# The last FFN's first batch: rows turned by VectorE's blocks instead of TensorE, projections and queries of the last attention batch spread anew

## The chip, the cores and the metric

One Trainium2 chip, one core of it. The kernel is one launch. The metric is device time in microseconds (us). The kernel before took 2222.87 us, the median of 4 runs that lay between 2220.93 and 2227.34 us. Besides these there is one profiled execution, whose trace all durations below are taken from.

The engines are called as the profile calls them: PE is TensorE (matrix products, transposes by a product with the identity), PEld its weight loads, DVE is VectorE, ACT is ScalarE, POOL is GpSimd, and SP issues most of the DMAs.

## The reference

Four layers with a layer norm behind each, on 8 batches of 512 rows of 512 numbers, all in float32:

```python
x = _layernorm(x + _L0_attn_ref(x, ...))   # 16 heads of 32, causal
x = _layernorm(x + _L0_ffn_ref(x, ...))    # 8 experts, the best 2 for each row
x = _layernorm(x + _L1_attn_ref(x, ...))   # 8 heads of 64, keys and values shared by 4 heads
x = _layernorm(x + _L1_ffn_ref(x, ...))    # gate, up and down by integer weights, hidden width 1408
```

The change lies at the seam of the last two. The attention of layer 1 ends with `x + out @ Wo.T`, a residual and a layer norm. The last FFN is

```python
W = (wq.astype(jnp.float32) - 128) * scale[:, None]
gate = silu(x @ Wg.T); up = x @ Wu.T
y = (gate * up) @ Wd.T
```

## The kernel before

**Layer 1's attention.** `Attention1.batches` runs batches 0 to 7 one after the other. A batch has 4 groups of two heads, and for each group 4 tiles of 128 keys, so 16 units, taken two at a time: 8 rounds, numbered 0 to 7. `plan(b)` (L1745) fills a list `todo` with the extra work of each round. A round is written in this order: scores of its two units (L1702, PE into `sc`, then the exponential on ACT, L1705, into `p`); the sums over the units of the round before (`add`, L1713, DVE: none for a group's first unit, `total<-p,p` for its second, `total<-total,p` for its third and fourth); the round's list; the products of the round before (`product`, L1724, PE into `av`). Behind every group's last product, so in rounds 2, 4, 6 and in round 0 of the next batch, comes `normalise` (L1729): PE sums the rows of `total` into `rs` (L1732), ACT copies them to `r_inv` (L995), DVE takes the reciprocal (L1735) and multiplies `av` with it (L1742, into `aoT`), and POOL adds `r_inv` to a running sum that guards the result (L998).

**The lists.** They hold the queries of the next groups (L1607), the output projection of the batch before, 128 rows at a time (`project`: PE L1670, DVE's residual L1676 and statistics L1684 and L1685; after the fourth tile POOL's `rstd`, L1688 and L1689), and the preparation of the next batch. The last batch, 7, has no next one. There the lists hold `split(0, c)` in rounds 0, 2, 4 and 6: it prepares the rows of batch 0 for the FFN. Their layer norm was done long before. `split` has 4 PE transposes of 128 x 128 (L1108), ACT's copy from PSUM to `x_high` (L1109), rounded to the type in which PE multiplies, and DVE's difference from PSUM to `x_low` (L1110). Queries 1, 2, 3 are in rounds 0, 1, 5, projections 0 to 3 of batch 6 in rounds 2, 3, 4, 7.

**Order.** In this stage the programs of PE, DVE, ACT and POOL are kept in the order in which they are written. Each engine takes its own instructions strictly in turn, so one that waits holds up all behind it on that engine. SP's DMAs are put in order by the scheduler.

**The tail.** After round 7 come the two last sums, the two last products, three of the four groups of projection 0 of batch 7, `normalise` of the last group, the remaining groups and projections, the norm of batch 6 and the residuals of batch 7.

**Turning rows otherwise.** Batches 2 to 7 of this attention, and batches 1 to 7 of the FFN, get their turned rows another way, `Turn`. DVE transposes 32 x 32 blocks (`blocks`, L88, one instruction of 128 x 512 for each tile of rows), four DMAs carry the result to DRAM (`out`, L93), and one brings it back (`back`, L96), all on SP's queue. For the next batch of the attention DVE's four instructions stand in round 3 and the first reader, the key product L1588, in round 6. Rows turned so come in another order of the 512 tokens; `by_tile` is the view that undoes this, in FFN by ACT's L1153 and DVE's L1154, which read `hT` in that view. FFN batch 0 reads plainly there, since `split` keeps the order.

**The FFN.** `IntegerFfn.batch` runs 11 hidden tiles in a batch: 8 + 8 products with `x_high` and `x_low` (L1143), then the halves of the hidden tile, then the output products (L1159). `parts` (L1094) makes the halves of later batches from the turned rows: ACT's copy and DVE's difference.

**Weights.** `weights.load` brings 2 units of the integer weights, `weights.convert` converts the pair before; both do nothing once `FIRST` = 20 units are on the core.

Of the kernel before, what the change touches and what calls it, by code (L numbers as in the profile page):

```python
# [9 lines left out]
F32 = mybir.dt.float32  # L10
# [4 lines left out]
ALU = mybir.AluOpType  # L15
# [3 lines left out]
P = 128  # L19
NB = 8  # L20
S = 512
D = 512
NT = S // P
ND = D // P
# [33 lines left out]
def in_order(tc, *engines):  # L58


    return tc.manual_schedule(engines={mybir.EngineType.PE, *engines})
# [11 lines left out]
class Turn:  # L73
# [11 lines left out]
    def blocks(self, room, t, x):  # L85

        out = room.rearrange("p (j t c) -> p j t c", t=self.n, c=32)[:, :, t, :]
        self.nc.vector.transpose(out, x.rearrange("p (j c) -> p j c", c=32))  # L88
# [708 lines left out]
class Tiles:  # L797
# [83 lines left out]
    def weights(self, i, c):  # L881
        at = self.ats[i]
        if i < N_FIXED:
            return self.w[:, at + c * 512 : at + (c + 1) * 512]
        return self.w[:, bass.ds(at + c * 512, 512)]
# [180 lines left out]
class IntegerFfn:  # L1066
# [13 lines left out]
        self.halves[b] = [pool.tile([P, ND, S], F32R, tag=f"rows{i}", name=f"x3_{part}")  # L1080
                          for i, part in enumerate(("high", "low"))]

    def blocks(self, b, t):

        if t == 0:
            self.room(b)
            self.turned = self.raw.tile([P, ND * S], F32, tag="turned", name="turned")
        turn = self.turns[b % 2]
        turn.blocks(self.turned, t, self.env.xs[b][:, t, :])
        if t == NT - 1:  # L1090
            turn.out(self.turned)
            turn.back(self.turned)

    def parts(self, b, c):  # L1094

        high, low = (half[:, c, :] for half in self.halves[b])
        x = self.turned[:, ts(c, S)]
        self.nc.scalar.copy(high, x)
        self.nc.vector.tensor_tensor(low, x, high.bitcast(F32), ALU.subtract)

    def split(self, b, c, ps):

        nc = self.nc
        if c == 0:
            self.room(b)
        high, low = self.halves[b]
        for t in range(NT):
            nc.tensor.transpose(ps[:, ts(t, P)], self.env.xs[b][:, t, ts(c, P)], self.env.ident)  # L1108
        nc.scalar.copy(high[:, c, :], ps)  # L1109
        nc.vector.tensor_tensor(low[:, c, :], ps, high[:, c, :].bitcast(F32), ALU.subtract)  # L1110

    def run(self, held_out, last_norm):
        tc, nc, weights = self.env.tc, self.nc, self.weights
# [21 lines left out]
    def hidden(self, b, c, held):  # L1135

        nc, vec, work, weights = self.nc, self.env.vec, self.work, self.weights
        g = self.p_gu.tile([P, S], F32, tag="g", name="ps_g1")
        u = self.p_gu.tile([P, S], F32, tag="u", name="ps_u1")
        for ps, w in ((g, weights(2 * c)), (u, weights(2 * c + 1))):  # L1140
            for dc in range(ND):
                for i, x in enumerate(self.halves[b]):
                    nc.tensor.matmul(ps, lhsT=w[:, ts(dc, P)], rhs=x[:, dc, :],  # L1143
                                     start=(dc, i) == (0, 0), stop=(dc, i) == (ND - 1, 1))
        sg = work.tile([P, S], F32, tag="sg", name="sg1", bufs=2)
        nc.scalar.activation(sg, g, AF.Silu, scale=vec[:, V_SG + c : V_SG + c + 1])
        hT = work.tile([P, S], F32, tag="hT", name="hT2", bufs=2)
        nc.vector.scalar_tensor_tensor(hT, u, vec[:, V_SU + c : V_SU + c + 1], sg, ALU.mult, ALU.mult)  # L1148
        high, low = (self.late.tile([P, S], F32R, tag=f"h{i}", name="h_late") if held else
                     work.tile([P, S], F32R, tag=f"h{i}", name="h_half", bufs=2) for i in range(2))  # L1150

        hT, *halves = [self.turns[0].by_tile(a, back) if b else a for a, back in ((hT, True), (high, False), (low, False))]
        nc.scalar.copy(halves[0], hT)  # L1153
        nc.vector.tensor_tensor(halves[1], hT, halves[0].bitcast(F32), ALU.subtract)  # L1154
        return high, low
# [381 lines left out]
class Attention1:  # L1537
# [94 lines left out]
        for part in (self.w_qkv[:, c, :], self.w_qkv[:, ND : ND + 2, ts(c, P)]):  # L1632
            self.nc.scalar.mul(part, part, self.nss[:, c : c + 1])

    def run(self, weights, split):

        with ExitStack() as phase:
            self.work = work = phase.enter_context(self.env.tc.tile_pool(name="c_work", bufs=1, reuse_waits="tile"))
            p_sc = phase.enter_context(self.env.tc.tile_pool(name="c_sc", bufs=2, space=PSUM, reuse_waits="tile"))
            p_av = phase.enter_context(self.env.tc.tile_pool(name="c_av", bufs=2, space=PSUM, reuse_waits="tile"))  # L1640
            with in_order(self.env.tc, mybir.EngineType.DVE, mybir.EngineType.Activation, mybir.EngineType.Pool):
                return self.batches(work, p_sc, p_av, weights, split)

    def batches(self, work, p_sc, p_av, weights, split):
        env, nc, guard, state, HD = self.env, self.nc, self.guard, self.state, self.HD
        xs = env.xs
        scale = 1.0 / math.sqrt(HD)
# [14 lines left out]
        def project(b, t):  # L1662
            ps = self.mm([P, D], "ps_o1")
            project_groups(b, t, ps, range(ND))
            residual(b, t, ps)
            statistics(b, t)
# [24 lines left out]
        def norm(b):  # L1691
            st = state.pop(b)
            for t in range(NT):
                x = xs[b][:, t, :]
                nc.vector.tensor_scalar(x, x, st["mv"][:, t, 0:1], st["rstd"][:, t : t + 1], ALU.subtract, ALU.mult)
# [49 lines left out]
        def plan(b):  # L1745


            todo = [[] for _ in range(ND * NT // 2)]
            here = pieces.pop(b)
            first, final = b == 0, b == NB - 1  # L1750
            if first:
                pieces[1] = self.prepare(1)
                todo[0] += [lambda t=t: pieces[1]["fetch"](t) for t in range(NT)]
            then = pieces.get(b + 1)
            if b:
                for t, i in enumerate((2, 3, 4, 7) if final else (2, 3, 4, 5)):
                    todo[i].append(lambda t=t: project(b - 1, t))
                if not final:
                    todo[6].append(lambda: norm(b - 1))
            for g, i in zip((1, 2, 3), (1, 3, 5) if first else (0, 1, 5) if final else (0, 1, 3)):  # L1760
                todo[i].append(lambda g=g: here["query"](g))
            if final:
                for c, i in enumerate((0, 2, 4, 6)):
                    todo[i].append(lambda c=c: split(0, c, self.mm([P, S], "ps_xT")))
            else:
                if first:

                    for t, i in ((2, 1), (3, 2)):
                        todo[i].append(lambda t=t: then["sum"](t))
                        todo[i + 2].append(lambda t=t: then["stat"](t))  # L1770
                for t, i in ((0, 1), (1, 2)) if first else ((0, 0), (1, 1), (2, 1), (3, 2)):
                    todo[i].append(lambda t=t: then["add"](t))
                if first:
                    todo[4].append(then["deviations"])

                    todo[5].insert(0, then["norm"])
                    todo[6] += [lambda c=c: then["turn"](c) for c in range(ND)]
                else:
                    todo[2].append(then["deviations"])
                    todo[3].append(then["norm"])  # L1780
                    todo[3] += [lambda t=t: then["blocks"](t) for t in range(NT)]
                todo[6].append(then["key"])
                todo[7] += [then["value"], lambda: then["query"](0)]
                if b + 2 < NB:
                    after = pieces[b + 2] = self.prepare(b + 2)
                    todo[7] += [lambda t=t: after["fetch"](t) for t in range(NT)]
            for i in (7,) if first else (1, 7) if final else (5, 7):
                todo[i] += [weights.convert, lambda: weights.load(work, 2, weights.FIRST)]
            return todo

        last = []
        for b in range(NB):
            for i, thunks in enumerate(plan(b)):
                units = [(b, u // NT, u % NT) for u in (2 * i, 2 * i + 1)]
                ps = [score(*unit) for unit in units]
# [12 lines left out]
        b = NB - 1  # L1808
# [16 lines left out]
def usual_pass(tc, ins, held_out):  # L1825
    nc = tc.nc
    with ExitStack() as ctx:
# [4 lines left out]
        with tc.tile_pool(name="a_mm", bufs=2, space=PSUM) as p_mm, ExitStack() as attn1_ctx:  # L1832
            with tc.tile_pool(name="routes", bufs=1, side="right") as routes, \
# [11 lines left out]
                attention = Attention1(env, guard, router, rows, own, p_mm, dram)  # L1845
# [15 lines left out]
            weights = IntegerWeights(env, guard)  # L1861
            weights.open(ctx.enter_context(tc.tile_pool(name="c_weights", bufs=1, side="right")), weights.FIRST)
            ffn = IntegerFfn(env, guard, weights, rows, dram)
            last_norm = attention.run(weights, ffn.split)
        ffn.run(held_out, last_norm)


# [236 lines left out]
def _layout(a):  # L2104
# [18 lines left out]
    def hidden(w):  # L2123
        return w.reshape(NHID, P, ND, P).transpose(0, 3, 2, 1).reshape(NHID, P, D)

    gate_up_q = np.stack([hidden(a["L1_ffn_wq_gate"]), hidden(a["L1_ffn_wq_up"])], axis=1).reshape(2 * NHID, P, D)

    def rows(n):
# [43 lines left out]
```

## Time and profile before

| what | value |
|---|---|
| median of 4 runs | 2222.87 us |
| profiled execution, its whole time | 2221.49 us |
| its span, first to last instruction | 2219.7 us |
| around the span | 1.8 us |
| granted TensorE clock, mean | 0.996 |
| last attention batch, round 0 to the first product of the FFN | 1635.90 to 1715.60 us |
| one FFN batch | about 63 us |

The span is what the trace shows; the time of a run is that and 1.8 us around it. Times in the trace are counted from the span's start. In the timeline a line begins with the start and the length of an instruction, or of several alike that follow each other ("x4"), then engine, line of the kernel, operation, output <- inputs, shapes, and in brackets how long the engine had been idle before and what released it.

Starts of the rounds of the last batch, by the first score product of each on PE (us):

| round | start | length | in its list |
|---|---|---|---|
| 0 | 1635.90 | 8.72 | query 1, split 0 |
| 1 | 1644.62 | 7.41 | query 2 |
| 2 | 1652.03 | 8.71 | projection 0, split 1 |
| 3 | 1660.74 | 7.42 | projection 1 |
| 4 | 1668.16 | 8.71 | projection 2, split 2 |
| 5 | 1676.87 | 7.42 | query 3 |
| 6 | 1684.29 | 5.23 | split 3 |
| 7 | 1689.52 | | projection 3 |

### The profile page before, as it was taken

What the parts mean: (1) busy time and instruction counts of PE and PEld (TensorE: products, weight loads), DVE (VectorE), ACT (ScalarE), POOL (GpSimd) and SP (SyncE); (2) the same over time, 40 slices, a digit from 0 to 9 for tenths busy, and PEclk for the clock granted to TensorE, in tenths of its full rate; (3) what the DMA queues carried; (4) which work ended last, traced back from release to release, by engine and by line L of the source; (5) the groups of instructions that cost most, each with busy time, mean ns of one, the idle gap of its engine ahead of it and who ended that gap; (6) DMA issues with size and microseconds to landing.
All of it is one profiled execution on the core that took longest, in us unless ns stands there. A gap on an engine that the chain in (4) does not pass through costs nothing. (4 is left out here: it accounts for less than half of the span.)

```text
span 2219.7 us, 23678 instructions
## 1 busy us (share of the span) xinstructions
PE 2183.9 (98%) x9006; PEld 1113.4 (50%) x9006; DVE 1275.1 (57%) x2032; ACT 631.8 (28%) x917; POOL 487.6 (22%) x489
## 2 busy tenths in 40 slices
PE   9999999999999999999999999999999999999997
PEld 3344444444444444444444334333343778888876
DVE  3556666666666643323317888788767654555443
ACT  2332323323233232122124233333232222222222
POOL 2332423224232343122105123221211000000000
PEclk9999999999999999999999999999999999999999
DMA  8010101101022216888635222322100321111000
GB/s 298 20 58 1 58 20 38 58 1 58 10 72 89 90 63 200 216 217 216 184 122 193 65 67 76 95 72 62 54 23 24 100 76 57 57 58 57 20 20 21
DMA packets 146428, 182.20 MB, mean 82 GB/s; under 512 B 60530, under 2 KB 89202, under 8 KB 144514
## 3 DMA queue, kind: packets, MB, share of 16 engines
q1 hardware_dynamic: 135024, 144.91, 20.9%
q0 software_dynamic: 10560, 34.61, 5.5%
q8 instruction: 74, 1.21, 0.2%
q10 hardware_dynamic: 722, 1.07, 0.1%
q14 instruction: 48, 0.39, 0.1%
HBM read 117.38 MB, written 63.18 MB: 81 GB/s over the span
## 5 line engine op out<-in xcount | busy, mean ns | idle before, releaser
L903 PE MATMUL ps_gu<-experts,xrT 128*128 128x512 f32 (+1 forms) x520 | 247.2, 598 | 0.0
L1360 ACT ACTIVATE p<-sc 128x2048 f32<-128x2048 f32 (+1 forms) x96 | 152.9, 1592 | 189.0 <-PE sc L1356 189.0
L1148 DVE SCALAR_TENSOR_TENSOR hT<-ps_u,vec,sg 128x512 f32<-128x512 f32 x88 | 65.6, 745 | 195.3 <-PE ps_u L1143 195.2
L1365 POOL TENSOR_SCALAR_AFFINE_SELECT p<-p 128x512 f32<-128x512 f32 x128 | 91.6, 730 | 380.8 <-ACT p L1360 377.3
L1159 PE MATMUL ps_f<-ffn_w,h_half 128*128 128x512 f32 x672 | 170.2, 393 | 0.6 <-issue 0.4
L998 POOL TENSOR_TENSOR g_total<-g_total,r_inv 128x512 f32<-128x512 f32 x64 | 89.7, 1401 | 358.9 <-DVE r_inv L1735 283.2
L1705 ACT ACTIVATE p<-sc 128x1024 f32<-128x1024 f32 x128 | 124.0, 1021 | 105.9 <-PE sc L1702 98.4
L1735 DVE RECIPROCAL r_inv<-r_inv 128x512 f32<-128x512 f32 x32 | 107.1, 3346 | 78.9 <-ACT r_inv L995 78.9
L1388 DVE TENSOR_TENSOR p<-p 128x1536 f32<-128x1536 f32 (+2 forms) x96 | 129.5, 1349 | 38.3 <-POOL p L1365 19.2
L905 DVE TENSOR_TENSOR h<-ps_gu,h 128x256 f32<-128x256 f32 x67 | 28.4, 425 | 209.0 <-ACT h L904 191.6
L1159 PEld LDWEIGHTS ps_f<-ffn_w,h_half 128*128 128x128 f32 x672 | 124.3, 188 | 33.0 <-DVE h_half L1154 5.5
L903 PEld LDWEIGHTS ps_gu<-experts,xrT 128*128 128x128 f32 x520 | 95.7, 196 | 89.3 <-issue 89.0
L1143 PE MATMUL ps_g<-x_high,ffn_w 128*128 128x512 f32 x352 | 138.8, 394 | 0.8 <-DVE x L1676 0.8
L1143 PE MATMUL ps_g<-x_low,ffn_w 128*128 128x512 f32 x352 | 139.1, 395 | 0.0
L1143 PE MATMUL ps_u<-x_low,ffn_w 128*128 128x512 f32 x352 | 138.8, 394 | 0.0
L1143 PE MATMUL ps_u<-x_high,ffn_w 128*128 128x512 f32 x352 | 138.6, 394 | 0.0
L919 PE MATMUL ps_y<-experts,hT 128*128 128x512 f32 (+1 forms) x272 | 127.9, 592 | 0.5 <-ACT hT L913 0.5
L1702 PE MATMUL sc<-qT,kT 64*128 64x512 f32 x512 | 127.2, 615 | 1.0 <-ACT qT L1609 0.7
L1292 PE MATMUL ps_q<-experts 128*128 128x512 f32 x256 | 120.3, 611 | 4.4 <-DMA experts<-in_xT 4.4
L1724 PE MATMUL av<-p,v 128*64 128x512 f32 x512 | 123.8, 605 | 0.0
L1285 PE MATMUL ps_v<-experts 128*128 128x512 f32 x256 | 116.3, 602 | 2.6 <-DVE v L1287 2.6
L1670 PE MATMUL ps_o<-attn_out,aoT 128*128 128x512 f32 x256 | 117.9, 604 | 0.8 <-ACT r_inv L995 0.8
(262 smaller groups left out, 3433.9 us busy)
## 6 DMA issues: line engine op xcount, KB each, us to landing
results<-y SPq DMA_DIRECT2D x68, 256.0 KB
turned<-turned SPq DMA_DIRECT2D x56, 256.0 KB
pair<-xrT SPq DMA_DIRECT2D x25, 512.0 KB
xrT<-pair SPq DMA_DIRECT2D x100, 128.0 KB
x<-in_x SPq DMA_DIRECT2D x8, 1024.0 KB
experts<-in_gate_up SPq DMA_DIRECT2D x8, 1024.0 KB
rows<-x SPq DMA_DIRECT2D x32, 256.0 KB
x<-rows SPq DMA_DIRECT2D x8, 1024.0 KB
```

Of the source, the lines that this page charges most:

```text
L903: nc.tensor.matmul(ps, lhsT=xT[:, c, :], rhs=self.weights(i, c), start=c == 0, stop=c == ND - 1)
L919: self.nc.tensor.matmul(ps, lhsT=hT[:, c, :], rhs=self.weights(i, ND + c), start=c == 0, stop=c == self.NI - 1)
L1143: nc.tensor.matmul(ps, lhsT=w[:, ts(dc, P)], rhs=x[:, dc, :], start=(dc, i) == (0, 0), stop=(dc, i) == (ND - 1, 1))
L1159: self.nc.tensor.matmul(os[t], lhsT=h[:, ts(t, P)], rhs=self.weights(2 * NHID + c), start=(c, i) == (0, 0), stop=(c, i) == (NHID - 1, 1))
L1285: nc.tensor.matmul(ps, lhsT=xts[b][:, c, ts(t, P)], rhs=wv[:, c, :], start=c == 0, stop=c == ND - 1)
L1292: nc.tensor.matmul(ps, lhsT=wq[:, g, ts(c, P)], rhs=xts[b][:, c, :], start=c == 0, stop=c == ND - 1)
L1360: nc.scalar.activation(p, sc[:, :, :width], AF.Exp, scale=scale)
L1388: nc.vector.tensor_tensor(total[:, :, P * kt :], total[:, :, P * kt :], p[:, :, at : at + w], ALU.add)
L1670: nc.tensor.matmul(ps, lhsT=state[b]["aoT"][:, c, ts(t, P)], rhs=w_out[:, c, :], start=c == 0, stop=c == ND - 1)
L1702: nc.tensor.matmul(sc[:, j, :], lhsT=st["kT"][hs, ts(kt, P)], rhs=st["qT"][g][hs, :], start=True, stop=True)
L1705: nc.scalar.activation(p, sc, AF.Exp, scale=scale)
L1724: nc.tensor.matmul(st["av"][HD * j : HD * (j + 1), :], lhsT=st["v"][:, kt, HD * j : HD * (j + 1)], rhs=p[:, j, :], start=kt == 0, stop=kt ...
```

## The change

In the last attention batch, `split` is gone. Its place is taken by the method of the later batches: DVE's four block transposes in round 3, SP's four DMAs out and one back into `turned2`, which takes the room of the batch's `hT` tile (last read by query 3), and `parts` for the four column blocks, two in round 6 and two in round 7. `parts` for batch 0 makes the difference on POOL instead of DVE, now from two operands in SBUF. Query 3 moves from round 5 to round 3, projections 2 and 3 from rounds 4 and 7 to rounds 5 and 6. The conversions and loads of weights are listed in rounds 0 and 1 instead of 1 and 7. FFN batch 0 reads its hidden tiles through `by_tile` like all others.

```diff
-    def blocks(self, b, t):
+    def blocks(self, b, t, room=None):
 
         if t == 0:
             self.room(b)
-            self.turned = self.raw.tile([P, ND * S], F32, tag="turned", name="turned")
+            self.turned = self.raw.tile([P, ND * S], F32, tag="turned", name="turned") if room is None else room
...
         self.nc.scalar.copy(high, x)
-        self.nc.vector.tensor_tensor(low, x, high.bitcast(F32), ALU.subtract)
-
-    def split(self, b, c, ps):
-
-        nc = self.nc
-        if c == 0:
-            self.room(b)
-        high, low = self.halves[b]
-        for t in range(NT):
-            nc.tensor.transpose(ps[:, ts(t, P)], self.env.xs[b][:, t, ts(c, P)], self.env.ident)
-        nc.scalar.copy(high[:, c, :], ps)
-        nc.vector.tensor_tensor(low[:, c, :], ps, high[:, c, :].bitcast(F32), ALU.subtract)
+
+        engine = self.nc.vector if b else self.nc.gpsimd
+        engine.tensor_tensor(low, x, high.bitcast(F32), ALU.subtract)
...
-        hT, *halves = [self.turns[0].by_tile(a, back) if b else a for a, back in ((hT, True), (high, False), (low, False))]
+        hT, *halves = [self.turns[0].by_tile(a, back) for a, back in ((hT, True), (high, False), (low, False))]
...
-                for t, i in enumerate((2, 3, 4, 7) if final else (2, 3, 4, 5)):
+                for t, i in enumerate((2, 3, 5, 6) if final else (2, 3, 4, 5)):
                     todo[i].append(lambda t=t: project(b - 1, t))
                 if not final:
                     todo[6].append(lambda: norm(b - 1))
-            for g, i in zip((1, 2, 3), (1, 3, 5) if first else (0, 1, 5) if final else (0, 1, 3)):
+            for g, i in zip((1, 2, 3), (1, 3, 5) if first else (0, 1, 3)):
                 todo[i].append(lambda g=g: here["query"](g))
             if final:
-                for c, i in enumerate((0, 2, 4, 6)):
-                    todo[i].append(lambda c=c: split(0, c, self.mm([P, S], "ps_xT")))
+
+                room = []
+                def blocks(t):
+                    if t == 0:
+                        room.append(self.own.tile([P, ND, S], F32, tag="hT", name="turned2"))
+                    ffn.blocks(0, t, room[0].rearrange("p k s -> p (k s)"))
+                todo[3] += [lambda t=t: blocks(t) for t in range(NT)]
+                for c, i in enumerate((6, 6, 7, 7)):
+                    todo[i].append(lambda c=c: ffn.parts(0, c))
...
-            for i in (7,) if first else (1, 7) if final else (5, 7):
+            for i in (7,) if first else (0, 1) if final else (5, 7):
                 todo[i] += [weights.convert, lambda: weights.load(work, 2, weights.FIRST)]
```

`attention.run` and `batches` get the whole `ffn` object instead of `ffn.split`.

## The prediction

> **What bounds the kernel now.** I read the page's first lines, then PE's waits from the last attention batches into the FFN, then the timeline of the last batch, round by round, on PE, DVE and POOL.
>
> ```profile
> span 2219.7 us, 23678 instructions
> ...
> PE 2183.9 (98%) x9006; PEld 1113.4 (50%) x9006; DVE 1275.1 (57%) x2032; ACT 631.8 (28%) x917; POOL 487.6 (22%) x489
> ...
> PE ps_g L1143 <- DVE x L1676: 0.8, 1, 0.8
> PE ps_o L1670 <- ACT r_inv L995: 0.8, 1, 0.8
> ```
>
> PE is busy all the time, and from 1560 to 1720 us it waits twice, 0.8 us each. So here only two things count: work taken from PE, and new waits of PE.
>
> ```profile
> 1635.90 1.99 PE L1702 MATMUL sc<-qT,kT 64*128 64x512 f32 x8
> 1637.82 3.70 PE L1607 MATMUL ps_q<-hT,attn_qkv 128*128 128x512 f32 x8
> 1641.36 0.60 PE L1108 MATMUL ps_xT<-ident,x 128*128 128x128 f32 x4
> 1641.89 1.94 PE L1724 MATMUL av<-p,v 128*64 128x512 f32 x8
> ...
> 1646.53 3.70 PE L1607 MATMUL ps_q<-hT,attn_qkv 128*128 128x512 f32 x8
> 1650.16 1.94 PE L1724 MATMUL av<-p,v 128*64 128x512 f32 x8
> ```
>
> From a query's start to the next product PE takes 4.07 us with four transposes between (1637.82 to 1641.89) and 3.63 without (1646.53 to 1650.16). Four transposes behind other work thus cost 0.44 us, though each is listed with 0.27: they are pipelined.
>
> **The change part by part.**
>
> *PE.* The rows for round lengths are: a score block up to the next work 1.92 (1635.90 to 1637.82), a filler 3.63, `av` to the next scores 1.87 without `rs` (1650.16 to 1652.03) and 2.73 with (1641.89 to 1644.62). So an even round with one filler takes 8.28, an odd one 7.41 as now, an even one with none 4.65. Round 3 gets projection and query together; batch 6's round 3 does the same and runs from 1590.10 to 1600.95, 10.85 us. New starts: round 1 at 1635.90 + 8.28 = 1644.18, round 2 at 1651.59, round 3 at 1659.87, round 4 at 1670.72, round 5 at 1675.37, round 6 at 1682.78, round 7 at 1691.06. Round 7 has no projection now: 1.91 for scores and 3.59 for the four `av` units (1695.06 to 1698.65), so the tail's first projection starts at 1696.56, and 2.77 later, at 1699.33, PE could begin the last `rs`. Before, it began at 1701.42. **PE's gain is 2.1 us.** As a cross-check the transposes alone give 3 x 0.44 + 0.58 (round 6: 5.23 less 4.65) = 1.9; the rest is one switch between kinds of work saved where two fillers stand together.
>
> *DVE.* Four differences from PSUM (0.67 each) go, four block transposes (2.48 together, batch 6's row below) come in round 3. They write over `hT`, so they wait for query 3, which ends 9.1 us after the round's start (batch 6: ACT copies it at 1599.19). DVE is through with projection 1's statistics at 8.2 (before: 1668.94 less 1660.74), so it idles 0.9, then transposes until 11.6 and sums (2.52) until 14.1. Behind it, `rs` of round 4 is due on PE at 10.85 + 1.92 + 1.77 = 14.54. Cost nothing, covered by 0.4 us; if the transposes also waited for ACT's copy of the query (0.58), 0.2 to 0.3.
>
> *SP.* Five more DMAs. No other DMA is issued between 1611.74 and 1714.91, so they are moved past nothing.
>
> ```profile
> 1601.70 2.48 DVE L88 STREAM_TRANSPOSE turned<-xn 128x512 f32<-128x512 f32 x4
> 1604.21 3.23 SPq L93 DMA_DIRECT2D turned<-turned  x4
> 1611.74 0.34 SPq L96 DMA_DIRECT2D hT<-turned  x1
> 1618.56 3.70 PE L1588 MATMUL ps_k<-hT,attn_qkv 128*128 128x512 f32 x8
> ```
>
> The same trip in batch 6: transposes end at 1604.18, the way back is issued at 1611.74, DMA traffic has died down by about 1616.2 (0.88 of the DMA engines' time from 1614 to 1616, 0.02 from 1616 to 1618). So 12 us. From 1659.87 + 11.6 the rows are back at 1683.5. ACT asks for them behind round 6's exponentials, at 1682.78 + 3.2 = 1686.0. Covered by 2.5 us.
>
> *ACT.* Four copies from SBUF (0.62, the FFN's row) for four from PSUM (0.59): nothing, ACT is idle most of each round. FFN batch 0's `by_tile` view costs nothing: L1153 takes 621 ns in batch 0 and 620 in batch 1, L1154 688 and 690.
>
> *The rest.* The weight lines do nothing in this batch already: the 1640 to 1710 list of DVE's work has no conversion. FFN begins when DVE's last residual frees PSUM (0.8 wait above); that stays.
>
> *POOL and the last sums.* Four differences of 128 x 512 on POOL, not in the trace before; nearest row the sum L998 with the same shapes, 1.27. POOL's order becomes: `rstd` (round 6), parts 0 and 1, L998, parts 2 and 3. What it runs beside matters:
>
> ```profile
> 1648.94 1.27 POOL L998 TENSOR_TENSOR g_total<-g_total,r_inv 128x512 f32<-128x512 f32 x1 [18.43 <-DVE r_inv L1735]
> 1648.97 0.69 DVE L1742 TENSOR_TENSOR aoT<-av,r_inv 128x512 f32<-128x512 f32 x1
> 1649.58 1.72 DVE L1713 TENSOR_TENSOR total<-p,p 128x1024 f32<-128x1024 f32 x1
> ...
> L1713 DVE TENSOR_TENSOR total<-p,p x32: 1215/1719/1733, 1164.2 to 1694.5; 128x1024 f32<-128x1024 f32 x32
> ...
> 1697.89 1.11 POOL L1688 TENSOR_SCALAR rstd<-mv 128x4 f32<-128x4 f32 x1 [2.77 <-DVE mv L1685]
> ```
>
> DVE's sum takes 1.22 at its fastest, but 1.72 in most cases, when it meets POOL's: it ends 1.09 after POOL's does, as if it began only then. The other way round, POOL's tiny L1688 (0.23 in the layer norm's row L182) takes 1.11 and ends with the DVE sum it met. So a POOL and a DVE operation on two SBUF operands run one after the other, and each meeting costs DVE 1.27 less an overlap of 0.13, about 1.1.
>
> The last chain on DVE: reciprocal of group 2 starts 0.89 after round 7 (1690.41 less 1689.52), the first sum ends at 6.60 (1696.12), the two last sums, now with no statistics between, at 9.1: 1691.06 + 9.1 = 1700.2, with 0.1 for the signal `rs` at 1700.3. PE, ready at 1699.33, waits 1.0. That much is without meetings. ACT's copies for parts 2 and 3 end at 3.8 and 4.4, POOL's L998 at 5.6. So part 2 stands ready at 5.65, while the first sum runs, gets its turn at 6.6, and the second sum waits; part 3 stands ready during the second, and the third waits. **Two meetings**: 1700.3 + 2.2 = 1702.5, 1.1 later than the old 1701.42. At the bounds: none, 1.1 earlier; one, as before. I take two, since POOL is always already waiting when a sum ends. The rest of the tail is unchanged behind `rs`.
>
> One rule of the Trainium skill speaks against this change: the page "SBUF — State Buffer", section "Who interferes with whom", holds that a VectorE instruction with two SBUF inputs and a GpSimd one that reads SBUF exclude each other, the later being held for the whole of the earlier. The rows agree but for the small overlap. Taken literally two whole operations of 1.27 would make the end 1.4 us later; without the rule it would be 1.1 earlier.
>
> **Sum.** -2.1 on PE, +1.0 for DVE's chain, +2.2 for two meetings: **+1.1 us**. Against the profiled execution, 2221.49, that is 2222.6; its time is 1.4 under the median, so the median becomes 2222.87 + 1.1 = **2224.0**.
>
> **Rivals.**
>
> *B, the sums win.* One meeting or none, or some of PE's gain survives: -2.1 (DVE's chain hidden after all) to 0, 2220.8 to 2222.9. For it: at 1699.01 DVE's next sum started 0.11 after the one that POOL's L1688 had met, so DVE is quick to go on. Against: L1688 was nearly nothing, and did go first.
>
> *C, the rows come back late (slower).* ACT takes its work in order: parts 0 and 1 hold up its copy of `rs` (due 1691.3), round 7's exponentials and so the whole last chain. ACT needs 1.24 for the two copies, so it decides once the rows land after 1690.0, 18.5 us after the transposes instead of 12. A trip of 24 us, twice the row, lands at 1695.4: 5.4 more, 2229.4. For it: nothing else hides the wait. Against: batch 6's trip with the same bytes, and no other traffic now.
>
> *D, a real gain.* Over 0.2% would need 4.4 us, but transposes (2.1) and both waits (1.6) make 3.7. Only something outside this batch could do it.
>
> *The new spread does nothing:* inside the forecast; moving fillers leaves PE's sum, as the round table shows.
>
> **How the numbers follow.** Forecast 0.50, B 0.30, C 0.13 (with it whatever else may hold ACT or the FFN's start), D 0.07. About 0.2%, 4.4 us, is what a measurement of this kernel can tell from no change: under 2218.4 is faster, over 2227.3 slower. Forecast and B both stay within: faster 0.07, same 0.80, slower 0.13. The range is B's end less 1.3 (the profiled run lies 1.4 under the median) to the forecast with 0.3 from round 4 and a third meeting (1.1), plus 1.3: 2219.5 to 2226.7. The forecast's own: 2222.9 to 2225.4.
>
> **What would show it.** No L1108 on PE; round 3 about 10.9 long, round 4 4.7; round 7's start near 1691. Right: POOL's differences lie between the last three L1713, two of which are 2.3 long, and PE waits 2 to 3.2 us ahead of the last `rs`. Wrong: those sums 1.2 long (B); ACT idle ahead of its first L1098 in round 6 for a DMA (C); a PE wait in round 4; or any shift in the FFN, whose 500 us should not move.

## The result and the profile after

The changed kernel takes 2227.09 us, the median of 42 runs, and the kernel before, timed beside it, 2224.46 us, the median of 66. The ratio is 1.0013, with a 95% interval of 1.0008 to 1.0017: slower by 2.9 us (1.8 to 3.8) by this ratio, and by 2.6 us by the medians. The forecast was 1.1 us slower, 2224.0 us and at most 2226.7. The direction was right, the size was not, and the time lies above the range. Of the 3.1 us between 2224.0 and 2227.09, 1.6 are not the change's: the forecast stood on 2222.87 us for the kernel before, the median of 4 runs, and 66 runs give 2224.46. Of the runs of the experiments below one is left out of its ratio, 5120.78 us of the kernel with its differences on DVE, whose ten others lie between 2224.46 and 2232.20 us.

The spans of the two profiled executions, 2219.7 and 2226.2 us, differ by more than the kernels do, so they are compared by stages. In the changed kernel round 0 of the last batch starts at 1638.41 us, 2.5 us later than before, although the two kernels do the same work up to there. That varies from execution to execution: in two profiles of one kernel, the one with 7 transposes below, round 0 starts at 1640.23 and at 1637.51 us. In the changed kernel PE's granted clock, as a share of full speed, is 0.93 from 700 to 800 us and 0.98 from 800 to 900, against 0.95 and 1.00 before, far ahead of the change. The FFN takes 504.3 us against 504.1. Between them, from round 0's first score product to the FFN's first product, it was 79.70 us (1635.90 to 1715.60) and is **83.47 us** (1638.41 to 1721.88). This way of 3.8 us more is what the change has to answer for.

First the waits of PE in the changed kernel from 1560 us to the end (engine, line, what it waited for, total, times, longest):

```profile
PE rs L1723 <- DVE total L1704: 2.9, 1, 2.9
PE ps_g L1134 <- DVE x L1667: 0.8, 1, 0.8
PE ps_o L1661 <- ACT r_inv L995: 0.8, 1, 0.8
...
```

(The two lines left out are of the FFN, 0.4 and 0.2 us.) The two waits of 0.8 us are the old ones. The new one is the one that was forecast, ahead of the last `rs`. (Lines have moved up by nine: L1723 was L1732, L1704 was L1713, L1661 was L1670.) The same end of the last batch in the kernel before, on PE, and its last two sums on DVE:

```profile
1701.42 1.08 PE L1732 MATMUL rs<-total,ones 128*64 128x512 f32 x4
1703.34 11.43 PE L1670 MATMUL ps_o<-attn_out,aoT 128*128 128x512 f32 x26 [0.84 <-ACT r_inv L995]
1715.60 0.50 PE L1143 MATMUL ps_g<-x_high,ffn_w 128*128 128x512 f32 x1 [0.84 <-DVE x L1676]
...
1697.71 2.52 DVE L1713 TENSOR_TENSOR total<-total,p 128x1024 f32<-128x1024 f32 x2
```

The timeline of the changed kernel from round 0 to the FFN, on PE:

```profile
1638.41 1.99 PE L1693 MATMUL sc<-qT,kT 64*128 64x512 f32 x8
...
1662.38 1.99 PE L1693 MATMUL sc<-qT,kT 64*128 64x512 f32 x8
...
1673.23 1.99 PE L1693 MATMUL sc<-qT,kT 64*128 64x512 f32 x8
...
1693.56 1.99 PE L1693 MATMUL sc<-qT,kT 64*128 64x512 f32 x8
1695.48 3.65 PE L1715 MATMUL av<-p,v 128*64 128x512 f32 x16
1699.06 2.84 PE L1661 MATMUL ps_o<-attn_out,aoT 128*128 128x512 f32 x6
1704.81 1.96 PE L1723 MATMUL rs<-total,ones 128*64 128x512 f32 x4 [2.90 <-DVE total L1704]
1707.60 13.44 PE L1661 MATMUL ps_o<-attn_out,aoT 128*128 128x512 f32 x26 [0.83 <-ACT r_inv L995]
1721.88 0.50 PE L1134 MATMUL ps_g<-x_high,ffn_w 128*128 128x512 f32 x1 [0.84 <-DVE x L1667]
```

Round 3 takes 10.85 us (1662.38 to 1673.23), and round 7 starts 55.15 us after round 0; the forecast said 10.85 and 55.16. The last `rs` starts 66.40 us after round 0, against 65.52 before (1701.42 less 1635.90): 0.9 us late. But what follows is longer too: the four products of `rs` take 1.96 us where they took 1.08, and the 26 of the projections 13.44 where they took 11.43. From `rs` to the FFN it was 14.18 us and is 17.07, **2.9 us more for the same instructions**. Busy time in four stretches, with the length, then PE, PEld, DVE, ACT and POOL, then PE's granted clock (1.00 is full speed), and last the share and the GB/s of the DMA engines:

```profile
1701.90:1704.80 2.90, 0.00 (x1) 0.02 (x1) 2.66 (x2) 0.00 (x0) 1.68 (x1) 1.00 0.00 0
1704.80:1707.60 2.80, 1.96 (x5) 0.30 (x5) 0.03 (x1) 0.69 (x2) 0.00 (x0) 0.51 0.00 0
1707.60:1711.20 3.60, 3.60 (x5) 1.53 (x6) 3.58 (x3) 0.00 (x0) 0.20 (x1) 0.50 0.00 0
1711.60:1721.80 10.20, 9.44 (x22) 3.80 (x20) 6.24 (x14) 0.00 (x0) 0.67 (x1) 1.00 0.00 0
```

From the end of the wait PE ran at half its clock for some 6.8 us. No term of the forecast stood for that.

The sums that PE waited for, on DVE and POOL of the changed kernel (DVE's lines, then POOL's):

```profile
1698.52 1.73 DVE L1704 TENSOR_TENSOR total<-p,p 128x1024 f32<-128x1024 f32 x1
1700.36 4.31 DVE L1704 TENSOR_TENSOR total<-total,p 128x1024 f32<-128x1024 f32 x2
...
1694.04 2.50 POOL L1101 TENSOR_TENSOR x_low<-turned,x_high 128x512 fp32r<-128x512 f32 x2
1697.89 1.28 POOL L998 TENSOR_TENSOR g_total<-g_total,r_inv 128x512 f32<-128x512 f32 x1 [1.34 <-DVE r_inv L1726]
1699.12 4.46 POOL L1101 TENSOR_TENSOR x_low<-turned,x_high 128x512 fp32r<-128x512 f32 x2
```

The two last sums take 4.31 us together instead of 2.52, and POOL's two differences 4.46 instead of the 2.50 that the first two took, most of it while DVE computed its reciprocal. Side by side, each engine holds the other up.

The rows came back in time: ACT's first L1098 starts at 1688.34, directly behind round 6's exponentials, without a wait.

### The profile page after: what moved, and what is told of

The parts are those of the page before. It is cut to its first block, busy times and chain, and to the rows that moved or that the text cites. A ratio compares the mean times of both kernels' runs of the same rounds, so it can differ in the third digit from the quotient of the medians.

```text
span 2226.2 us, 23664 instructions
## 1 busy us (share of the span) xinstructions
PE 2188.6 (98%) x8990; PEld 1112.9 (50%) x8990; DVE 1275.3 (57%) x2032; ACT 631.9 (28%) x917; POOL 492.7 (22%) x493
## 5 line engine op out<-in xcount | busy, mean ns | idle before, releaser
L1661 PE MATMUL ps_o<-attn_out,aoT 128*128 128x512 f32 x256 | 119.9, 613 | 0.8 <-ACT r_inv L995 0.8
```

What stands on the lines that cost most here:

```text
L1661: nc.tensor.matmul(ps, lhsT=state[b]["aoT"][:, c, ts(t, P)], rhs=w_out[:, c, :], start=c == 0, stop=c == ND - 1)
```

## The experiments

Called M here: POOL's two differences meet the last sums of DVE, PE idles for it, and the idle costs clock. Rivals are R (the loss is in the round trip to DRAM, in POOL as such, or in the FFN) and S (the new spread is what costs). In each trace three things are read: PE's wait ahead of the last `rs`, the way from that `rs` to the FFN's first product, and the whole stretch from round 0 to that product.

**The meetings taken away.** Against the changed kernel:

```diff
-                for c, i in enumerate((6, 6, 7, 7)):
+                for c, i in enumerate((6, 6)):
                     todo[i].append(lambda c=c: ffn.parts(0, c))
...
         project_groups(b, 0, banks[0], range(ND - 1))
         sums[-1]()
+        for c in (2, 3):
+            ffn.parts(0, c)
```

> The changed kernel with parts 2 and 3 of the rows moved from round 7 to behind the last group's normalise in the tail. Theory M (two POOL differences meet the last DVE sums, PE idles 2.9 us, and that idle halves PE's clock for some 6 us): the last two sums take 2.5 us together instead of 4.3, PE waits about 1.0 us ahead of the last rs, the granted clock stays at 1.00 in the tail, and round 0 to the FFN's first product takes about 78.6 us (before 79.7, changed kernel 83.5). Time about 1.1 us under the kernel before. Rival R (the loss lies in the round trip, the new spread of the lists or the FFN): the time stays some 2.6 us over the kernel before.

Measured: ratio 0.9996 (0.9987 to 1.0005), medians 2224.17 and 2224.76 us. The two sums on DVE in its timeline:

```profile
1700.77 1.72 DVE L1704 TENSOR_TENSOR total<-p,p 128x1024 f32<-128x1024 f32 x1
1702.60 2.55 DVE L1704 TENSOR_TENSOR total<-total,p 128x1024 f32<-128x1024 f32 x2
```

PE waits 1.15 us, the clock stays at 1.00, the stretch is 78.81 us. `parts` is a cast on ACT and a difference on POOL, so two of each have moved, and with them the whole loss is gone. The time can't be told from that of the kernel before, though the stretch is 0.9 us shorter. R falls: the round trip, POOL's first two differences and the `by_tile` views are all still there.

**The filler put back.** Against the changed kernel:

```diff
-                for t, i in enumerate((2, 3, 5, 6) if final else (2, 3, 4, 5)):
+                for t, i in enumerate((2, 3, 5, 7) if final else (2, 3, 4, 5)):
```

> The changed kernel with projection 3 put back from round 6 into round 7 (2, 3, 5, 7), nothing else. Theory M: PE has 3.6 us of work again between round 7's scores and its products, and POOL's rstd, which waits for the statistics of that projection, holds parts 2 and 3 back behind the last sums. So the sums take 2.5 us, PE doesn't wait ahead of the last rs, the clock stays at 1.00, and the whole 2.1 us of the transposes remain: round 0 to the FFN's first product about 77.6 us, time about 2.1 us under the kernel before. Rival R (round trip, POOL at all, or the FFN): still 2 us or more over the kernel before.

Measured: ratio 0.9987 (0.9978 to 0.9996), medians 2221.81 and 2224.76 us: faster than the kernel before, and, by the intervals of the two ratios, than the changed one. Its PE lines and POOL's beside them:

```profile
1699.78 2.84 PE L1661 MATMUL ps_o<-attn_out,aoT 128*128 128x512 f32 x6
1702.55 1.08 PE L1723 MATMUL rs<-total,ones 128*64 128x512 f32 x4
1704.47 11.43 PE L1661 MATMUL ps_o<-attn_out,aoT 128*128 128x512 f32 x26 [0.84 <-ACT r_inv L995]
...
1700.21 2.06 POOL L1680 TENSOR_TENSOR rstd<-rstd,neg_half 128x4 f32<-128x4 f32 x1
1702.24 2.48 POOL L1101 TENSOR_TENSOR x_low<-turned,x_high 128x512 fp32r<-128x512 f32 x2
```

No wait ahead of `rs`, which starts 63.42 us after round 0 (1639.13), 2.1 us earlier than before; the stretch is 77.60 us, as expected. POOL's differences start at 1702.24, when the sums are over, since `rstd` stands ahead of them in POOL's order. So the gain of 2.1 us on PE is real, and round 7's projection was what protected it: as work for PE, and by holding POOL back. This run doesn't tell the two apart.

**The new spread alone.** Against the kernel before, transposes on TensorE kept:

```diff
-                for t, i in enumerate((2, 3, 4, 7) if final else (2, 3, 4, 5)):
+                for t, i in enumerate((2, 3, 5, 6) if final else (2, 3, 4, 5)):
...
-            for g, i in zip((1, 2, 3), (1, 3, 5) if first else (0, 1, 5) if final else (0, 1, 3)):
+            for g, i in zip((1, 2, 3), (1, 3, 5) if first else (0, 1, 3)):
```

> The kernel before with the new spread alone: queries in rounds 0, 1, 3 and projections in rounds 2, 3, 5, 6, TensorE's transposes kept. Theory M: round 7 has no filler any more, so PE comes to the last rs about 0.9 us ahead of DVE's sums and waits that long; no POOL meeting, no clock loss. Round 0 to the FFN's first product about 80.4 us, time about 0.7 us over the kernel before. Rival S (the spread is what costs): the wait is near 3 us and the time 2 us or more over the kernel before.

Measured: ratio 1.0003 (0.9994 to 1.0012), which says no more than that it is small. The trace says it better: a wait of 1.15 us, full clock, a stretch of 80.71 us, 1.0 us over the kernel before. So S holds for that 1 us alone.

**The differences on DVE.** Against the changed kernel:

```diff
-        engine = self.nc.vector if b else self.nc.gpsimd
+        engine = self.nc.vector
```

> The changed kernel with the four differences of the FFN's first batch on DVE instead of POOL. Theory M: no meeting, but two differences of 0.69 us stand ahead of the last sums, so PE waits about 2.3 us ahead of the last rs. If the clock falls only after an idle near 2.9 us, it stays at 1.00 and the time is about 0.2 us over the kernel before; if 2.3 us is enough, the tail runs at half clock for some us and the time is about 3 us over. Rival R: the same as the changed kernel, 2.6 us over, at full clock.

Measured: ratio 1.0013 (1.0004 to 1.0022). PE waits 2.09 us, and here too the clock falls to 0.50: 17.07 us from `rs` to the FFN, a stretch of 82.65 us. None of POOL's differences is in this kernel, so the clock's loss hangs on the wait, not on the meetings. An idle "near 2.9 us" is not needed.

**The wait by itself.** The kernel before, with n block transposes on DVE ahead of the last two sums, which nothing reads (n = 4, 7, 12):

```diff
+        pad = self.own.tile([P, ND, S], F32, tag="hT", name="pad")
+        for i in range(n):
+            self.turn.blocks(pad.rearrange("p k s -> p (k s)"), i % NT, xs[0][:, i % NT, :])
         for unit in last:
             add(*unit)
```

> The kernel before with 4 extra DVE block transposes (2.5 us, into the free room of the last batch's hT tile, read by nobody) ahead of the last two sums, nothing else. PE then waits about 1.4 us ahead of the last rs. Theory G (an idle of PE of 2 us and more brings half clock for some 6.5 us, which costs a fixed 2.9 us): clock 1.00, round 0 to the FFN's first product 81.1 us, time 1.4 us over the kernel before. Rival H (the half clock after the change had to do with POOL or DVE traffic): the same.

> The same with 7 block transposes: PE waits about 3.2 us. Theory G: half clock for about 6.5 us behind the wait, round 0 to the FFN's first product 79.7 + 3.2 + 2.9 = 85.8 us, time about 6 us over the kernel before. Rival H: clock 1.00, 82.9 us, 3.2 us over.

> The same with 12 block transposes: PE waits about 6.3 us. Theory G: the loss by the clock is no larger than with 3.2 us, so 79.7 + 6.3 + 2.9 = 88.9 us and about 9 us over the kernel before. Rival K (the loss by the clock grows with the idle time): twice the clock's loss, near 92 us. Rival H: 86.0 us at clock 1.00.

Measured: ratios 1.0015 (1.0005 to 1.0025), 1.0013 (1.0003 to 1.0023) and 1.0055 (1.0038 to 1.0071). With 7 the trace is as G said: 2.97 us wait, 17.09 us behind it, 85.65 us in all. With 12 the wait is 5.93 us and the way behind it 16.70, so the loss doesn't grow with the idle time, and K falls. H falls as well: it expected full clock here, where POOL has no new work.

With 4, however, G is wrong: the wait is only 1.19 us, and the clock still falls, though 2.4 us after the wait and for only half as long. The traces show why. In each of the twelve, PE's clock changes only at points that lie whole multiples of 3.41 us apart. Cut at these points, the tail of this kernel reads as the first three lines, and that of the new spread alone, with nearly the same two waits of PE, as the last two:

```profile
1705.45:1708.87 3.42, 1.58 (x5) 0.49 (x6) 1.47 (x2) 0.69 (x2) 0.00 (x0) 1.00 0.00 0
1708.87:1712.28 3.41, 3.41 (x5) 1.35 (x4) 3.38 (x3) 0.00 (x0) 0.50 (x1) 0.50 0.00 0
1712.28:1715.69 3.41, 3.41 (x9) 1.52 (x8) 3.36 (x9) 0.00 (x0) 0.77 (x1) 1.00 0.00 0
...
1700.68:1704.09 3.41, 2.26 (x8) 0.62 (x7) 2.50 (x3) 0.00 (x0) 0.00 (x0) 1.00 0.00 0
1704.09:1707.50 3.41, 2.58 (x9) 1.06 (x6) 2.08 (x1) 0.69 (x2) 0.00 (x0) 1.00 0.00 0
```

With 4 transposes both waits, ahead of `rs` and behind it, fall into one window: PE idles 3.42 less 1.58, 1.84 us of it, and half clock follows. In the other kernel a boundary lies between the waits, the windows have 1.15 and 0.83 us idle, and the clock stays. So it is in this stage of all twelve traces. Half clock followed every window with 1.84 us idle or more and none with 1.15 or less; 1.82 us, once, did not bring it (with 12 transposes, just ahead of a window that was idle throughout). It went on behind windows with 0.78 to 1.44 us idle and ended behind those with 0.10 or less, which makes one or two windows, 3.4 or 6.8 us.

The timed runs fit no simple sum: the median with 7 is no higher than with 4, though its profile is 3.5 us longer, and the two intervals overlap almost wholly. With 7 the time is 0.7 to 5.1 us over the kernel before, where G expected about 6.

**Is it always so?** The changed kernel twice more and the 7 transposes once more, one profile each:

> The changed kernel once more, one profile. What is asked: is the loss by the clock behind the last rs there in every execution? Theory F (it depends on where the wait falls for the clock's control, so it comes by chance): the wait of 2.9 us ahead of the last rs is the same, and the way from that rs to the FFN's first product takes either 14.2 us at clock 1.00 or up to 17.1 us with half clock. Theory G (fixed): always 17.1.

> The same again, with the same expectations: under theory F not all looks alike, under theory G 17.1 us each time.

> The kernel before with 7 extra block transposes ahead of the last sums, once more: a wait of 3.0 us ahead of the last rs. Theory F: 14.2 to 17.1 us from that rs to the FFN's first product, not bound to the 17.1 us of the first look. Theory G: 17.1 again.

Measured: waits of 2.9, 2.9 and 3.0 us, ways of 17.06, 16.82 and 17.17 us, half clock in all three, whole stretches of 83.45, 83.21 and 85.72 us. So a wait near 3 us lost the clock in five profiles of five. That doesn't exclude F. By the windows above, a wait of 2.90 us does no harm where a boundary leaves at most 1.83 us of it on either side. That is 0.76 us of 3.41, an estimate of about one execution in five; no trace caught one.

All of it in one table. "At half clock" is twice the clock time that windows of 0.5 us from 4 us before the `rs` show as not granted. "Most idle" is PE's longest idle time in one window between points where the clock can change.

| kernel | wait ahead of the last `rs`, us | most idle, us | `rs` to FFN, us | at half clock, us | round 0 to FFN, us |
|---|---|---|---|---|---|
| before | none | 0.84 | 14.18 | 0 | 79.70 |
| changed | 2.90 | 2.90 | 17.07 | 6.8 | 83.47 |
| changed, two more profiles | 2.9 | 2.90, 2.43 | 17.06, 16.82 | 6.8 | 83.45, 83.21 |
| differences on DVE | 2.09 | 2.09 | 17.07 | 6.8 | 82.65 |
| parts 2, 3 in the tail | 1.15 | 1.15 | 14.17 | 0 | 78.81 |
| spread alone | 1.15 | 1.15 | 14.17 | 0 | 80.71 |
| projection 3 in round 7 | none | 0.84 | 14.18 | 0 | 77.60 |
| before + 4 transposes | 1.19 | 1.84 | 15.88 | 3.4 | 82.66 |
| before + 7 transposes, two profiles | 2.97, 3.0 | 2.43, 2.33 | 17.09, 17.17 | 6.8 | 85.65, 85.72 |
| before + 12 transposes | 5.93 | 3.41 | 16.70 | 6.8 | 88.22 |

## Why the prediction was wrong, step by step

*PE's gain of 2.1 us:* right. Round 7 starts at 55.15 us, predicted 55.16, and with the filler back the whole 2.1 us show at the end.

*DVE's block transposes, SP's DMAs, ACT's copies, `by_tile`:* right, they cost nothing. PE waits nowhere before the tail, and C, the late rows, didn't occur.

*DVE's chain as the new bound, +1.0 us:* right. Without meetings PE waits 1.15 us.

*Two meetings of POOL and DVE, +2.2 us:* two there were. They cost 1.8 us (4.31 less 2.52), 0.9 each instead of 1.1. So the sum up to the last `rs`, +1.1, measured +0.9. The rule of the Trainium skill that was weighed (page "SBUF — State Buffer", section "Who interferes with whom") points the right way. Its literal price, the whole of each operation, would be 2.5, an estimate from two of 1.27 us.

*"The rest of the tail is unchanged behind `rs`":* **this step failed.** It set the instructions behind the wait at their old lengths. They take 2.9 us more, since the granted clock is 0.50 for 6.8 us. Less the 0.2 by which the sum up to `rs` came out lower, that is the whole difference between the forecast's +1.1 and the +3.8 us of the profile. The forecast expected the wait of 2 to 3.2 us in so many words, and gave it only its own length. Its signs of being right came true, from round 3 to the unmoved FFN; none of them was PE's clock in the tail.

In this stage the trace of before shows no such loss: with waits of 0.8 us the clock stays at 1.00. But it holds one elsewhere, behind a wait of 1.77 us (a line of PE, then a stretch):

```profile
719.72 1.15 PE L1356 MATMUL sc<-q,k 32*128 32x384 f32 x16 [1.77 <-ACT p L1360]
...
721.70:725.11 3.41, 3.21 (x16) 1.11 (x19) 2.92 (x19) 1.19 (x1) 1.22 (x2) 0.50 0.02 5
```

One page speaks of it: the Trainium skill, "TensorE: Matmul & The Clock Gate", section "Part 1: The HAM clock gate (the "warmup" mystery)", holds that the clock is halved when PE has been idle over a window of 3.4 us, and that these windows run on their own, not from the kernel's start. The size of the windows agrees with the traces' 3.41 us, and a start of their own with the boundaries, which lie elsewhere in each execution. The condition doesn't agree: here 1.84 us idle in one window were enough. So the length of a wait alone doesn't decide; what counted in this stage is how much idle time fell into one window, which a wait of 1.19 us reached together with one of 0.84. That was found in the traces afterwards. No run moved a wait of one length on purpose, and idle time isn't the whole condition either: in the trace of before, half clock also followed the window from 735.35 to 738.76 us, which has only 0.46 us idle.

*The time.* The stretch says +3.8 us in one profile, +3.7 and +3.5 in two more, the runs +2.9 (1.8 to 3.8). If one execution in five escapes the clock's loss, as estimated above, the mean would be near 0.9 + 0.8 x 2.9 = 3.2. Whether some do stays open: of the changed kernel's executions, those with a mean granted clock of 0.993 or less lie about 2228, those with 0.995 or more about 2224 us, which would fit, but the kernel before shows clocks of 0.993 to 0.997 too, and no trace was taken of such a run.

## What to carry to other kernels

Where one engine is the bound, a change that takes work from it must be followed to the places where that work was cover: here a gain of 2.1 us on PE laid bare a chain on DVE, and moving one projection by one round decides between 0.13% slower and 0.13% faster. A new wait of the matrix engine is not priced by its length alone: in this stage a wait of 2 us or more cost another 2.5 to 3.0 us by the clock, and one of 1.19 us, with one of 0.84 us close behind it, 1.7. And work that is handed to POOL "for free" isn't, if it is due just when DVE runs two-operand sums on the chain that ends last; an instruction ahead of it in POOL's own order can hold it back without costing anything.

## What the runs showed of the hardware

In the tail PE's clock fell to 0.50 behind single waits of 2.09 us and more, and behind 1.19 and 0.84 us that together put 1.84 us of idle time into one window of 3.41 us; it stayed there for 3.4 or 6.8 us. Behind a wait of 5.93 us the loss was no larger than behind 2.09. POOL and DVE, each with operations on two SBUF operands in a row, took turns: two of 1.25 and two of 1.26 us took 4.46 and 4.31 us side by side.
